# Cross-attention and mixture-of-experts kernel: how the setup fetches the head scales and the key and query weights, and when GpSimd clears the values' tiles

## The chip, the cores and the metric

The kernel runs on one core of one Trainium2 chip. The metric is the device time of one execution in microseconds (us); the time before is the median of three runs. The profile is one further execution, recorded by the hardware profiler, with times counted from the start of its span.

## The reference, cut to what matters

`x` is (4, 1024, 256), the context (4, 77, 256), the head values `f` are (4, 16), one number for each batch and head.

```python
def xattn(ctx, x_normed, f):               # 16 heads of 64
    k, v = split(layernorm(ctx, ln1_w, ln1_b) @ Wkv)
    q = layernorm(x_normed, ln2_w, ln2_b) @ Wq
    q = q * (1 + f[:, None, :, None]) + f[:, None, :, None]
    a = softmax(q k^T / 8)                 # by batch and head, over the 77 keys
    return (a v) @ Wout

x = x + xattn(ctx, norm(x), f)
x = x + experts(norm(x))                   # 9 experts, top 2 of a softmax router
```

All arithmetic is float32.

## The kernel before, in words

The order of the instructions on each engine is the order in which the program writes them down; the framework adds the waits on semaphores. Nothing is reordered by a scheduler. So an instruction that waits holds up everything written after it on the same engine.

The work has three stages. The **setup**, from 0 to about 67 us, folds the weights into per-batch matrices: `g` (queries' and keys' weights and the normalised context, so that scores come straight from the normalised tokens) and `u` (values times the output weights). The **attention** stage then runs over 32 sub-tiles of 128 tokens, and the **experts'** stage over blocks of token lists. The change touches only the first 27 us of the setup.

What the setup does there, by engine and line:

- SyncE issues the transfers of the context `cx` (L384, two halves), the keys' weights `wk_sb` and the queries' weights `wq_sb` (L389, two transfers each, one for each half of the 1024 columns), the values' weights `wv_sb` (L390) and the output weights `wo_sb` (L391). They run on queue q1.
- ScalarE issues, on queue q10, the two rows of the context's norm weights `crows` (L361), then `fs` (L367), the 64 head values copied to all 128 partitions, and later `wrow` (L476). Its arithmetic here is small roots, a quarter of `cn`, and one half of `cT` (L504).
- GpSimd clears and sends a few small tiles, then clears `vbd` (L590, 128 x 4096), `vrem` (L597) and parts of `u` (L599). An added dependency makes the clearing of `vbd` wait for the last instruction that writes the normalised context `cn` (L466) on VectorE. Iotas and small clears follow.
- TensorE runs eight warm-up products on zeros (L159) in two parts, turns `crows` (L424, into `pc`), and turns the normalised context `cn` into two tiles `pct` (L495), one for each half `c` of the 256 channels.
- VectorE takes the statistics of `cx` (L410, L412), makes `cn` (L466) and `cwb` (L475), copies `fs` into `shift` with two instructions, one for even and one for odd heads (L484), makes `scale1` and `shift` of it (L486, L487), clears `cfold` (L489), and then writes the second half of `cT` (L499), the normalised and weighted context. In the text `cT` has two halves: `c = 0` is ScalarE's (L504), `c = 1` is VectorE's (L499).
- The key loop (L512 to L529) has 8 blocks `n`. Each makes `pk` = `wk_sb` x `cT` in a PSUM bank, with two products (`c = 0` and `c = 1`) that the profile shows as two records each. ScalarE copies it to `kT` (L519) and VectorE multiplies it with `scale1` into `kTs` (L520). From block 4 on, TensorE also turns a quarter of `wq_sb` (L434, `pwq`) and VectorE multiplies it with `wrow` (L447).
- Then come `pcq` (L537), 32 products `pgk` (L651), and the values' part, in which `vbd` and `vrem` are written from `pv` (L724) and used by `pu` (L739) and `pur` (L745).

PSUM has 8 banks of 512 floats in a partition. `bank_tile` gives them out in turn, so a product has to wait until the tile eight places before it has been read.

## Time and profile before

| what | value |
|---|---|
| time before, median of 3 runs | 930.13 us (929.72 to 930.16) |
| the profiled execution | 929.22 us, of which its span 927.2 us |
| mean granted TensorE clock over the span | 0.994 |
| TensorE busy | 907.9 us (98% of the span) |
| VectorE, ScalarE, GpSimd busy | 453.3, 341.6, 318.9 us |
| chain of work that ended last | TensorE 87%, DMA 5%, issue 3%, VectorE 2% |
| VectorE waits for `fs` | 2.1 us, once |
| TensorE waits at `pk` (L515) | 2.6 us for `wk_sb`, 2.5 us behind VectorE's L489 and L499 |
| first `pk` products start | 10.11 us (the first two records), 13.41 us (all others) |

The profiled execution lies 0.91 us under the median. The line numbers are those of the kernel before. A busy share is a mean over stages; in the stretch that the change touches, TensorE is idle for several microseconds. "Idle before" in a timeline is the time that an engine had nothing running ahead of the instruction, with what released it.

### The profile page before, as it was taken

Reading aid. Unit: us, or ns where it says so; the run is one execution under the profiler, and the core shown is the slowest. Engines: PE = TensorE matmul, PEld = TensorE weight load, DVE = VectorE, ACT = ScalarE, POOL = GpSimd, SP = SyncE. Lnnn points to the kernel's source line nnn. Section 1 sums busy time; section 2 is a strip of 40 time slices with the busy share of each in tenths; the row PEclk is TensorE's granted clock in tenths of the full one; section 3 lists DMA queues with packets and bytes.
Section 4 is the critical chain, followed back from the end, with each engine's and each line's share of the span. In section 5 each row is a group of like instructions: output and inputs, shape, how many; then the busy total and the mean of one; then the engine's idle time right before and its main releaser. Section 6 shows DMA issues by size and latency. Waiting matters only on the chain.

```text
span 927.2 us, 13369 instructions
## 1 busy us (share of the span) xinstructions
PE 907.9 (98%) x4208; PEld 704.1 (76%) x4208; DVE 453.3 (49%) x1331; ACT 341.6 (37%) x1075; POOL 318.9 (34%) x329
## 2 busy tenths in 40 slices
PE   7999999999999999999999999999999999999996
PEld 5676767777777777788887777777778778778885
DVE  5777678788888977853632222222222222222221
ACT  2667565755656575551111222222222111112210
POOL 5000000412404151246544435435435435444422
PEclk8999999999999999999999999999999999999998
DMA  6100010503012610446869779779779777779822
GB/s 216 48 23 1 1 69 24 35 35 46 24 46 62 220 46 24 117 121 168 213 187 294 210 211 307 216 204 312 222 212 308 225 213 213 226 216 311 233 33 23
DMA packets 109747, 137.05 MB, mean 148 GB/s; under 512 B 24357, under 2 KB 79149, under 8 KB 109678
## 3 DMA queue, kind: packets, MB, share of 16 engines
q1 hardware_dynamic: 92042, 118.78, 41.6%
q0 software_dynamic: 17344, 17.26, 10.4%
q8 instruction: 34, 0.56, 0.3%
q14 instruction: 35, 0.29, 0.1%
q10 hardware_dynamic: 292, 0.17, 0.1%
HBM read 119.51 MB, written 18.33 MB: 149 GB/s over the span
## 4 chain that ended last, share of the span: by engine, by line
PE 87%; DMA 5%; issue 3%; DVE 2%; ACT 1%; POOL 1%; SPq 0%; POOLq 0%; ACTq 0%
PE pg L1193 21%; PE po L1267 16%; PE po L338 15%; PE psc L261 14%; PE pa L319 3%; PE psg L1229 3%; PE psu L1229 3%; PE psb L1229 2%; DMA out_dram<-co,ids 2%; PE px L1179 2%; PE pu L739 1%; PE pk L515 1%; PE ph L1250 1%; DMA wd_r<-in_L_ffn_Wd_dram 1%; PE pgk L651 1%
## 5 line engine op out<-in xcount | busy, mean ns | idle before, releaser
L1193 PE MATMUL pg<-xT,wgu 128*128 128x256 f32 x1144 | 251.7, 379 | 0.4 <-DMA wd_r<-in_L_ffn_Wd_dram 0.4
L1193 PEld LDWEIGHTS pg<-xT,wgu 128*128 128x128 f32 x1144 | 215.9, 190 | 29.3 <-issue 0.8
L1267 PE MATMUL po<-wd,hid 128*128 128x256 f32 (+1 forms) x804 | 180.5, 379 | 0.0
L1267 PEld LDWEIGHTS po<-wd,hid 128*128 128x128 f32 (+1 forms) x804 | 147.2, 187 | 21.3 <-issue 0.7
L275 ACT ACTIVATE ex<-psc,mx 128x77 f32<-128x77 f32 x512 | 124.1, 361 | 102.2 <-DVE mx L265 98.0
L1302 POOL DMA_INDIRECT out_dram<-co,ids x63 | 100.7, 1598 | 172.3 <-DVE co L1270 133.2
L918 POOL DMA_INDIRECT list_d<-r_entry,r_pli x64 | 68.2, 1065 | 255.4 <-issue 125.4
L338 PE MATMUL po<-u,aT 128*128 128x265 f32 x640 | 151.7, 391 | 0.9 <-ACT aT L327 0.6
L261 PE MATMUL psc<-g,zT 128*128 128x462 f32 (+1 forms) x384 | 139.1, 511 | 1.2 <-ACT zT L250 1.2
L338 PEld LDWEIGHTS po<-u,aT 128*128 128x128 f32 x640 | 118.7, 189 | 23.7 <-ACT aT L327 1.9
L1200 DVE TENSOR_TENSOR hid<-pg,sl 128x256 f32<-128x256 f32 x130 | 55.1, 425 | 160.1 <-ACT sl L1199 160.0
L1199 ACT ACTIVATE sl<-pg 128x256 f32<-128x256 f32 x130 | 49.8, 384 | 218.3 <-PE pg L1193 213.2
L261 PEld LDWEIGHTS psc<-g,zT 128*128 128x128 f32 x384 | 72.5, 189 | 59.2 <-issue 49.4
L1270 DVE TENSOR_SCALAR co<-po,ids 128x256 f32<-128x256 f32 x67 | 32.4, 484 | 136.0 <-PE po L1267 133.7
L1151 POOL DMA_INDIRECT yin<-y_d,ids x67 | 70.3, 1049 | 23.8 <-issue 15.1
L265 DVE TENSOR_REDUCE mx<-psc 128x6 f32<-128x462 f32 (+1 forms) x96 | 55.7, 581 | 17.9 <-PE psc L261 15.3
L295 DVE TENSOR_REDUCE sm<-ex 128x16 f32<-128x1232 f32 x32 | 45.9, 1435 | 37.0 <-ACT ex L275 37.0
L327 ACT COPY aT<-pa 128x512 f32<-128x512 f32 (+1 forms) x96 | 49.4, 552 | 26.4 <-PE pa L319 26.4
L319 PEld LDWEIGHTS pa<-ident,an 128*128 128x128 f32 x320 | 36.9, 141 | 7.7 <-PE po L338 1.4
L319 PE MATMUL pa<-ident,an 128*128 128x128 f32 x320 | 40.2, 273 | 1.0 <-DVE an L299 1.0
L299 DVE TENSOR_TENSOR an<-ex,rs 128x1024 f32<-128x1024 f32 x32 | 39.2, 1225 | 1.1
L1255 ACT COPY hid<-ph 128x384 f32<-128x384 f32 x15 | 7.2, 479 | 73.9 <-PE ph L1250 73.9
(310 smaller groups left out, 845.6 us busy)
## 6 DMA issues: line engine op xcount, KB each, us to landing
wgu<-in_L_ffn_Wg_dram SPq DMA_DIRECT2D x41, 704.0 KB
wd<-in_L_ffn_Wd_dram SPq DMA_DIRECT2D x41, 640.0 KB
wgu<-in_L_ffn_Wu_dram SPq DMA_DIRECT2D x41, 512.0 KB
wgu<-in_L_ffn_Wu_dram SPq DMA_DIRECT2D x41, 128.0 KB
x<-in_x_dram SPq DMA_DIRECT2D x8, 512.0 KB
out_dram<-x SPq DMA_DIRECT2D x8, 512.0 KB
y_d<-y SPq DMA_DIRECT2D x8, 512.0 KB
w<-in_L_ffn_Wg_dram SPq DMA_DIRECT2D x5, 704.0 KB
```

The source lines that it names most:

```text
L261: nc.tensor.matmul(psc[:, :w], zT[:, c, :], g_sb[i // NS // GPB][:, c, h * J : h * J + w], start=(c == 0), stop=(c == C - 1),)
L265: nc.vector.tensor_reduce(nmx[i][:, h : h + n], psc[:, : n * J].rearrange("p (h j) -> p h j", h=n), AX.X, ALU.max, negate=True,)
L275: nc.scalar.activation(exs[i][:, h + q, :], pscs[k][:, q * J : (q + 1) * J], AF.Exp, bias=nmx[i][:, h + q : h + q + 1],)
L319: nc.tensor.transpose(pa[:, q * P : (q + 1) * P], ans[i][:, (k + q) * P : (k + q + 1) * P], ident)
L338: nc.tensor.matmul(po[:, :DE], aT[:, n, :], u_sb[b][:, n, :], start=(n == 0), stop=(n == KC - 1))
L918: i = nc.gpsimd.indirect_dma_start(out=list_d[:, :], out_offset=bass.IndirectOffsetOnAxis(ap=place_i[:, s : s + 1], axis=0), in_=entries[k ...
L1151: return nc.gpsimd.indirect_dma_start(out=dst, out_offset=None, in_=src, in_offset=bass.IndirectOffsetOnAxis(ap=offsets, axis=0), **kw,)
L1193: nc.tensor.matmul(pg[:, g, :], w[:, c, at : at + P], xT[:, c, :], start=(c == 0), stop=(c == C - 1),)
L1200: nc.vector.tensor_tensor(hid[:, f, :], pg[:, 1, :], sl, ALU.mult)
L1229: nc.tensor.matmul(pgs[k][rows, :n], xT[:, c, rows], w[:, c, at : at + n], start=(c == 0), stop=(c == C - 1),)
L1267: nc.tensor.matmul(po[rows, :D], hid[:, f, at], d[:, f, :], start=(f == 0), stop=(f == NF))
L1302: i = nc.gpsimd.indirect_dma_start(out=out_r, out_offset=bass.IndirectOffsetOnAxis(ap=rows_of(j, h, rows), axis=0), in_=cos[j][:, h, :], i ...
```

## The change

It edits the setup in four places.

1. The transfer `fs` to 128 partitions goes. In its place ScalarE's queue brings `frows`, two partitions (even heads, odd heads) of 32 numbers each, picked from DRAM with a step of two numbers; it is issued ahead of the first activation instead of behind it. VectorE makes a small tile `two` from the identity matrix, and TensorE makes `pfs` = `two` x `frows`, which puts the head values on all 128 partitions in PSUM. `scale1` and `shift` are then made straight from `pfs`.
2. `scale1`, `shift` and the clearing of `cfold` move on VectorE from ahead of the second half of `cT` to behind it; the two copies of L484 go. `pfs` takes one turn of the PSUM banks between `pct` and `pk`.
3. `wk_sb` and `wq_sb` come in one transfer each, with rows of 1024 numbers in place of 512.
4. The clearing of `vbd` on GpSimd, and with it what follows there, waits for the second half of `cT` (L499) in place of the last of `cn` (L466).

```diff
+        frows = kside.tile([2, B, NP], F32, name="frows")
...
+        nc.scalar.dma_start(out=frows, in_=fside.rearrange("b (n t) -> t b n", t=2))
...
-        fs = vside.tile([P, B, NP, 2], F32, name="fs")
-        nc.scalar.dma_start(
-            out=fs.rearrange("p b n t -> p (b n t)"),
-            in_=fside.rearrange("(o b) h -> o (b h)", o=1).to_broadcast([P, B * H]),
-        )
...
-        wk_v = wkv[:, :INNER].rearrange("(c p) n -> p c n", p=P)
-        for dst, src in ((wk_sb, wk_v), (wq_sb, wq_v)):
-            for k in range(2):
-                at = slice(2 * k * quarter, 2 * (k + 1) * quarter)
-                nc.sync.dma_start(out=dst[:, :, at], in_=src[:, :, at])
+        nc.sync.dma_start(out=wk_sb, in_=wkv[:, :INNER].rearrange("(c p) n -> p c n", p=P))
+        nc.sync.dma_start(out=wq_sb, in_=wq_v)
...
+        two = kside.tile([2, 2, P // 2], F32, name="two")
+        nc.vector.tensor_copy(two, ident[:2, :2].unsqueeze(2).to_broadcast([2, 2, P // 2]))
...
-                normed = nc.vector.tensor_scalar(
+                nc.vector.tensor_scalar(
                     cn[:J, b, :], cx[:J, b, :], cmv[:J, b, 0:1], cr[:J, b : b + 1],
...
-        shift = kside.tile([P, NP, B], F32, name="shift")
-        scale1 = kside.tile([P, NP, B], F32, name="scale1")
-        for t in range(2):
-            half = slice(64 * t, 64 * t + 64)
-            nc.vector.tensor_copy(shift[half], fs[half, :, :, t].rearrange("p b n -> p n b"))
-        nc.vector.tensor_scalar(scale1, shift, ATT_SCALE, ATT_SCALE, ALU.mult, ALU.add)
-        nc.vector.tensor_scalar(shift, shift, ATT_SCALE, None, ALU.mult)
-        cfold_all = kside.tile([P, NP, P // QT], F32, name="cfold")
-        nc.vector.memset(cfold_all, 0.0)
...
-                nc.vector.tensor_scalar(
+                normed = nc.vector.tensor_scalar(
                     cT[:, c, :], pt[:, : B * J], cwb[:, c, 0:1], cwb[:, c, 1:2],
...
+        pfs = bank_tile("pfs")
+        nc.tensor.matmul(
+            pfs[:, : B * NP], two.rearrange("r t p -> r (t p)"),
+            frows.rearrange("r b n -> r (b n)"), start=True, stop=True,
+        )
+        heads = pfs[:, : B * NP].rearrange("p (b n) -> p n b", b=B)
+        nc.vector.tensor_scalar(scale1, heads, ATT_SCALE, ATT_SCALE, ALU.mult, ALU.add)
+        nc.vector.tensor_scalar(shift, heads, ATT_SCALE, None, ALU.mult)
+        cfold_all = kside.tile([P, NP, P // QT], F32, name="cfold")
+        nc.vector.memset(cfold_all, 0.0)
```

More of the change, by code (lines that the diff above doesn't have):

```diff
@@ L478 @@
         )
-        shift = kside.tile([P, NP, B], F32, name="shift")
-        scale1 = kside.tile([P, NP, B], F32, name="scale1")
-        for t in range(2):
-            half = slice(64 * t, 64 * t + 64)
-            nc.vector.tensor_copy(shift[half], fs[half, :, :, t].rearrange("p b n -> p n b"))
-        nc.vector.tensor_scalar(scale1, shift, ATT_SCALE, ATT_SCALE, ALU.mult, ALU.add)
-        nc.vector.tensor_scalar(shift, shift, ATT_SCALE, None, ALU.mult)
-        cfold_all = kside.tile([P, NP, P // QT], F32, name="cfold")
-        nc.vector.memset(cfold_all, 0.0)
-        cfold = cfold_all[:, :, : 2 * B].rearrange("p n (t b) -> p n t b", t=2)
         for c in range(C):
@@ L507 @@
                 )
+        shift = kside.tile([P, NP, B], F32, name="shift")
+        scale1 = kside.tile([P, NP, B], F32, name="scale1")
+        pfs = bank_tile("pfs")
[8 more added lines that the diff above has]
+        nc.vector.memset(cfold_all, 0.0)
+        cfold = cfold_all[:, :, : 2 * B].rearrange("p n (t b) -> p n t b", t=2)
         TURN = NP - NP // 2
```

## The prediction, on record before the changed kernel ran

> **What bounds the kernel now.** I read the page first, then TensorE's waits, then the chain of waits over the setup, then the timeline of the first 20 us, then its windows with clock and DMA. The page says that TensorE is the bound as a mean:

> ```profile
> PE 907.9 (98%) x4208; PEld 704.1 (76%) x4208; DVE 453.3 (49%) x1331; ACT 341.6 (37%) x1075; POOL 318.9 (34%) x329
> ```

> TensorE's waits, longest first, show where the missing 2% lie. The two longest are both at the first key products; the rest of the list is 1.5 us of start-up and 4.0 us spread over the kernel.

> ```profile
> PE pk L515 <- DMA wk_sb<-in_L_xattn_Wkv_dram: 2.6, 1, 2.6
> PE pk L515 <- DVE cfold L489: 2.5, 1, 2.5
> ```

> The chain over the setup (start, duration, what) says what ends there last: the transfer of `fs`, four small VectorE instructions, then TensorE without a break to 66.66 us.

> ```profile
> 1.69 7.38 DMA fs<-in_fside_Bx_dram
> ...
> 9.10 1.38 DVE shift L484
> 10.49 0.92 DVE shift L484
> ...
> 11.44 0.94 DVE scale L486
> ...
> 12.41 0.92 DVE shift L487
> ...
> 13.41 7.17 PE pk L515 x18
> 20.58 0.44 PE pwq L434 x4
> ```

> The timeline shows why such small instructions take 0.9 us each:

> ```profile
> 6.94 3.51 POOL L590 MEMSET vbd<- 128x4096 f32 x1 [1.38 <-DVE cn L466]
> 10.39 0.99 POOL L597 MEMSET vrem<- 128x1024 f32 x1
> 11.32 1.97 POOL L599 MEMSET u<- 128x1060 f32 x2
> ...
> 12.77 0.56 DVE L499 TENSOR_SCALAR cT<-pct,cwb 128x308 f32<-128x308 f32 x1
> ```

> VectorE's four end at 10.48, 11.41, 12.38 and 13.33; GpSimd's first two clears end at 10.45 and 11.38, the last at 13.29, and the pair's middle is 12.3. Each small instruction ends when a clear ends. The same kind of work without a clear beside it is short: L556 on 64x32 takes 0.18 us at 29.50. `cT` (c = 1) could have been written from 7.53, when `pct` was turned, but stands behind them and ends at 13.33.

> The windows (length, then busy times, clock, DMA share, GB/s) give the clock: it falls to half at about 11.1 and is back at about 18.0.

> ```profile
> 10.00:11.00 1.00, 0.76 (x2) 0.30 (x2) 0.99 (x2) 0.00 (x0) 1.00 (x2) 1.00 1.06 408
> 11.00:12.00 1.00, 0.00 (x0) 0.00 (x0) 0.96 (x2) 0.00 (x0) 1.00 (x2) 0.57 1.06 404
> ...
> 17.00:18.00 1.00, 1.00 (x3) 0.66 (x2) 0.48 (x1) 0.31 (x1) 0.00 (x0) 0.51 0.70 240
> 18.00:19.00 1.00, 1.00 (x5) 0.72 (x5) 0.00 (x1) 0.42 (x1) 0.00 (x0) 1.00 0.38 129
> ```

> At half clock a `pk` record comes every 0.51 us (weight loads at 14.09, 14.60, 15.11); at full clock every 0.26 (chain: 1.04 for 4).

> **The change, part by part.**

> *Removed from VectorE's path.* The wait for `fs` until 9.07 and the four instructions from 9.10 to 13.33. `cT` (c = 1) now starts when `pct` is turned (7.53) and takes 0.56: ready at 8.1. ScalarE's half is ready at 7.91 as before. `scale1` and `shift` come behind it; at 0.18 each they end near 8.6, and if they too had to sit out the clear of `vbd` and then `vrem`, near 12.7. That costs nothing either way: the first reader is `kTs` of block 0, and TensorE needs the bank of `pfs` back only eight tiles after it, at the second `pwq`, some 7 us into the products.

> *Added.* `two`: about 0.18 us, in VectorE's 0.36 us wait for ScalarE's root (5.18 to 5.54); were it held by GpSimd to 5.56, `cT` would be 0.2 later, which the next item hides. `pfs`: two small records, 0.2 us (as L424's) on an idle TensorE. Its wait for `frows` is the one that matters: all `pk` products stand behind it. Issued ahead of the activation, it delays the root's table load by 0.4 us, with 2.1 us of idle ScalarE behind it.

> *When `frows` lands.* No row shows a picked transfer of single numbers on this queue. The trace's landing marks (semaphore steps, one for each DMA engine that takes part) are 16 for a transfer to 128 partitions, 11 for `cx` (77 partitions), 1 for a row of `crows`; so two partitions will use one or two engines, 32 numbers or more each, where `fs` had 8 packets. `crows` landed at 3.56. `fs` landed engine by engine from 3.78 to 9.07, the first half of `wk_sb` from 5.68 to 9.98. The late engines are late for both queues, so they start late; they aren't slow at `fs`. Once going, a packet on this queue takes 15 ns (51 packets for 4.9% of 16 engines between 3 and 4 us), and one of `wk_sb` 82 ns (162 for 82.9% between 8 and 9). Twenty-four numbers more than `fs`, each perhaps behind one packet of weights, add 0.4 to 2.4 us: 4.2 at the earliest, 11.5 on the latest engine. I take 8.6, a middle engine (6.2 + 2.4).

> *The weights in one transfer.* TensorE had the first half at 10.11 (marks to 9.98), the second half landed by 11.37. Now block 0 needs all of it. If the number of packets set the pace, the whole lands like the first half, 9.98; if bytes do, like the second, 11.37 less what `fs` took; at 12.7 if one more half's time (1.34) is lost. Between 9 and 13 us the DMA moved 401 to 411 GB/s, whatever the packets' size, so bytes count late; before 8 us it moved at most 231, so there something else does. I take 11.0, near the bytes' end. `wq_sb` is needed by `pwq`, 6 us after the start; its last mark was 15.21: hidden. It would cost only beyond 17.

> *GpSimd* starts to clear at 8.15 instead of 6.94 and is done at 16.6 instead of 15.42. `vbd` is first written from `pv`, after 38.5; `numbers` reads the iotas in the thirties: hidden by 20 us. Nothing is queued behind it until the `z` clears, which wait for `pb` at 37.

> *The sum.* Products start at max(8.1, `pfs` at 8.8, 11.0) = 11.0 and are 20 records instead of 18, because none runs ahead. TensorE is then idle from 7.53 (bar `pfs`) to 11.0. With the clock's steps where this profile has them (half from 11.1; the next step up one interval earlier, 14.56, since 11.14 to 17.97 is two equal intervals of 3.41 and the first is now full), 7 records run to 14.56 and 13 more take 3.4: `pwq` at 17.95 instead of 20.58, 2.6 us earlier. From there TensorE's chain has no gap to 66.66, all else in the setup is driven by it, and it waits 4.0 us in all for the rest of the kernel, so the 2.6 us pass to the end. The profiled execution of 929.22 us would be 926.6; it lies 0.91 under the median of 930.13, and on the median the forecast is 927.5 us.

> With 9.98 as the start, `pwq` comes at 16.9 (gain 3.7); with 11.4 at 18.15 (2.4); with 12.7 at 18.9 (1.7).

> **The rivals.** *The clock takes the gain.* TensorE's idle stretch ends earlier, but the clock may stay at half for two intervals after the new start, 11.0 to 17.97: 13.6 records by then, 6.4 at 0.26, `pwq` at 19.6, gain 0.95: 929.2 us. For it: the steps need not fall where this profile has them. Against: the interval before (14.56 to 17.97) was full and did release the clock. [...]

> *The clock never falls*, because 3.5 us of idleness cover no whole interval: 20 records at 0.26 from 11.0, `pwq` at 16.2, gain 4.4: 925.7 us. Against: an interval with 0.76 us of work in it let the clock fall here.

> *The weights come late*, 12.5 to 12.7: gain 1.9 to 1.7, 928.2 to 928.4, as worked out above.

> *`frows` is late: slower.* The products stand behind a transfer of single numbers on few engines. Products from 12.9 on give no gain (10 records at 0.51 to 17.97, 10 at 0.26 to 20.58); with `pfs` 0.2, that is a landing at 12.7, or 0.29 us for each of 32 numbers after 3.56. At 0.45 us each they land at 18.0; `pwq` comes at 25.1, 4.5 us later: 934.6 us. For it: `fs` needed up to 7.0 us for 8 packets on an engine, 0.87 each. Against: the late engines' time was start-up, and 15 ns is the packet's own time. [...]

> That the change doesn't do what it says I give no chance of its own: the removed row on the chain is plainly replaced.

> **How the numbers follow.** Forecast case (weights between 9.9 and 12.4, one interval at half clock) 0.58, gain 1.9 to 3.7; clock never falls 0.07; clock takes the gain 0.17; weights late 0.07; `frows` late 0.11. What a measurement of this kernel can tell from no change is about 0.2%, 1.9 us. Faster by more than that: 0.58 + 0.07 = 0.65; within: 0.17 + 0.07 = 0.24; slower: 0.11. The range reaches from a gain of 4.2 (start at 9.5, or most of the case in which the clock stays up) to one of 0.2, below the case of the clock: 925.9 to 929.9. It leaves out the late `frows` and the tails.

> **What would show it.** Right: the chain over the setup without `fs` and without L484 to L487; `cT` (c = 1) done at about 8.1; the clear of `vbd` starting just after; TensorE's wait at `pk` put down to `wk_sb` until about 11; half clock for about 3.4 us; first `pwq` near 18 us; later stages shifted as a whole. Wrong: a long wait of TensorE at `pfs` for `frows`; `scale1` ending with the clear of `vbd` would only show that a PSUM source doesn't free VectorE from GpSimd; half clock until 18 would show the clock's rival; a gain at `pwq` that is gone at 67 us would mean that a wait in the values' part took its place.

## The result, and the profile after

The changed kernel took 925.42 us (median of 6 runs, 924.44 to 926.78). All six runs of before that stood beside it give 929.47 us (928.38 to 930.16), so the ratio is 0.9958 with an interval of 0.9945 to 0.9971: 4.05 us faster. The forecast was 927.5 us. Of the 2.1 us between the two, 0.7 is the base (the three runs of before shown ahead had a median of 930.13), and 1.4 is a gain larger than the 2.6 us that the sum gave. The profiled execution of the changed kernel took 924.82 us with a span of 922.8: 4.4 us less than that of before.

The page's row of TensorE in the changed kernel: two records more (`pfs`), 1.2 us less of busy time, and the same 98% share.

```profile
PE 906.7 (98%) x4210; PEld 703.5 (76%) x4210; DVE 450.0 (49%) x1330; ACT 341.7 (37%) x1075; POOL 318.2 (34%) x329
```

TensorE's waits of the changed kernel (us, times, longest): where two waits of 2.6 and 2.5 us stood at the first key products, one is left, and it is the weights'.

```profile
PE pk L515 <- DMA wk_sb<-in_L_xattn_Wkv_dram: 1.8, 1, 1.8
```

The timeline of the changed kernel (start, duration, engine, line, what, and in brackets the idle time before it and its releaser):

```profile
7.73 0.70 PE L479 MATMUL pct<-ident,cn 77*128 77x77 f32 x8
...
8.36 0.40 PE L497 MATMUL pfs<-frows,two 2*128 2x32 f32 x2
8.47 0.60 DVE L483 TENSOR_SCALAR cT<-pct,cwb 128x308 f32<-128x308 f32 x1 [1.11 <-PE pct L479]
8.98 0.18 DVE L503 TENSOR_SCALAR scale<-pfs 128x32 f32<-128x32 f32 x1
...
9.13 3.51 POOL L590 MEMSET vbd<- 128x4096 f32 x1 [3.56 <-DVE cT L483]
...
10.60 5.42 PE L515 MATMUL pk<-cT,wk_sb 128*128 128x308 f32 x20 [1.83 <-DMA wk_sb<-in_L_xattn_Wkv_dram]
...
15.85 0.60 PE L431 MATMUL pwq<-ident,wq_sb 128*128 128x128 f32 x4
```

`pfs` waits for nothing, `cT` (c = 1) starts the moment the last `pct` is done, `scale1` takes 0.18 us, the clear of `vbd` comes behind `cT`, and the products wait for `wk_sb` alone. They start at 10.60. Twenty records then take 5.42 us, 0.27 each, and the first `pwq` starts at 15.85. In before's timeline that row is:

```profile
20.42 0.60 PE L434 MATMUL pwq<-ident,wq_sb 128*128 128x128 f32 x4
```

So it comes 4.57 us earlier. The first scores start at 62.80 for 67.37, again 4.57, and the last product `pg` of the experts at 909.00 for 913.40, 4.40: the gain is made before 16 us and passes to the end.

The windows of the changed kernel (length, busy PE, PEld, DVE, ACT, POOL, then the granted clock, the DMA share and GB/s) over the stretch where before's clock stood at half:

```profile
11.00:12.00 1.00, 1.00 (x6) 0.72 (x5) 0.00 (x0) 0.09 (x1) 1.00 (x1) 1.00 1.03 408
...
17.00:18.00 1.00, 1.00 (x7) 0.77 (x7) 0.77 (x3) 0.47 (x2) 0.51 (x15) 1.00 0.51 170
```

The clock is 1.00 in both and in those between, where before's was 0.57 falling to 0.50 until 18. The half clock that the forecast charged didn't come in this execution. The six times fall into two groups: 924.44, 924.65 and 924.82 with a mean granted clock of 0.997 to 0.998, and 926.03, 926.38 and 926.78 with 0.995 to 0.996. The profiled execution belongs to the first; the second is taken up under the experiments.

### The profile page after: what moved, and what is told of

Its sections match the earlier page's. It is cut to its first block, busy times and chain, and to the rows that moved or that the text cites. A ratio compares the mean times of both kernels' runs of the same rounds, so it can differ in the third digit from the quotient of the medians.

```text
span 922.8 us, 13371 instructions
## 1 busy us (share of the span) xinstructions
PE 906.7 (98%) x4210; PEld 703.5 (76%) x4210; DVE 450.0 (49%) x1330; ACT 341.7 (37%) x1075; POOL 318.2 (34%) x329
## 3 DMA queue, kind: packets, MB, share of 16 engines
q0 software_dynamic: 17344, 17.26, 10.5%
## 5 line engine op out<-in xcount | busy, mean ns | idle before, releaser
L265 DVE TENSOR_REDUCE mx<-psc 128x6 f32<-128x462 f32 (+1 forms) x96 | 55.7, 581 | 18.1 <-PE psc L261 15.1
```

The costliest lines, as they stand in the source:

```text
L265: nc.vector.tensor_reduce(nmx[i][:, h : h + n], psc[:, : n * J].rearrange("p (h j) -> p h j", h=n), AX.X, ALU.max, negate=True,)
```

## The experiments

Gains are against the runs of before that stood beside each kernel on the same chip; the brackets hold the ratio's interval. Lines of these kernels are shifted by a few against those of the two kernels shown.

**Before, in the new order.** The block of `shift`, `scale1` and `cfold` goes behind `cT`; `fs`, the halves and the early clears stay.

```diff
-        for t in range(2):
-            nc.vector.tensor_copy(shift[half], fs[half, :, :, t]...)
-        nc.vector.tensor_scalar(scale1, shift, ...)
-        nc.vector.tensor_scalar(shift, shift, ...)
         for c in range(C):
             ...cT...
+        for t in range(2):
+            nc.vector.tensor_copy(shift[half], fs[half, :, :, t]...)
+        nc.vector.tensor_scalar(scale1, shift, ...)
+        nc.vector.tensor_scalar(shift, shift, ...)
```

> The kernel before, with one thing of the change: the making of shift, scale1 and the clear of cfold stands on VectorE behind the second half of cT. The fs transfer, the halves of the weights and GpSimd's early clears stay. Theory A (start of the key products, then clock): cT is ready near 8.1 us, the products start when the first half of the key weights lands (10.0 to 10.1 instead of 13.4); the small instructions still end with the clears (10.5 to 13.3), hidden by the PSUM banks. Gain 3.4 us less the 0.5 us of two records that ran ahead, plus 0 to 2.5 us of clock: 924.5 to 926.5 us against 929.5, no slower than the whole change. Rival B (VectorE has to be free of GpSimd, so the later clears are needed): kTs of block 0 comes after 13.4 and TensorE stalls for banks, less than 1 us gained. Rival C (the gain comes from fewer, longer transfers): no gain, 929.5 us.

Measured: 923.67 us against 928.84, 5.2 less, 0.9947 [0.9934, 0.9959], somewhat more than the 3.0 to 5.0 that theory A gave it. Its timeline:

```profile
6.98 3.51 POOL L590 MEMSET vbd<- 128x4096 f32 x1 [1.42 <-DVE cn L466]
...
9.08 0.60 DVE L487 TENSOR_SCALAR cT<-pct,cwb 128x308 f32<-128x308 f32 x1 [2.09 <-PE pct L483]
9.59 1.85 DVE L501 COPY shift<-fs 64x32 f32<-64x32 f32 x2
9.96 5.42 PE L515 MATMUL pk<-cT,wk_sb 128*128 128x308 f32 x20 [0.92 <-DMA wk_sb<-in_L_xattn_Wkv_dram]
...
11.48 0.93 DVE L503 TENSOR_SCALAR scale<-shift 128x32 f32<-128x32 f32 x1
```

The copies and `scale1` are still as long as in before (two in 1.85 us, one in 0.93), but TensorE doesn't wait for them now. `cT` reads PSUM and takes 0.60 us in the middle of the clear of `vbd`. The order alone gives all that the change gave, and the products start at 9.96, when the first half of the weights is there. That the product from `pfs` or the whole transfers were needed for the gain falls.

**Before, with late clears.** Only the instruction that the clear of `vbd` waits for is another: `cT` in place of the last `cn`.

```diff
-                normed = nc.vector.tensor_scalar(
+                nc.vector.tensor_scalar(
                     cn[:J, b, :], ...
...
-                nc.vector.tensor_scalar(
+                normed = nc.vector.tensor_scalar(
                     cT[:, c, :], ...
```

> The kernel before, with one thing of the change: GpSimd's clear of vbd waits for the second half of cT. Order on VectorE, fs and the halves stay. Theory A: after fs lands (9.07 us) the four small instructions take 0.2 us each instead of 0.9, cT is ready near 10.5, the products run from then: gain 2.9 us plus 0 to 2.5 us of clock, 924.5 to 926.7 us. Rival B' (the wait for fs is what counts, the blocking is not real and the instructions are slow by themselves): cT at 13.3 as before, no gain, 929.5 us. Rival C (transfers): no gain.

Measured: 922.64 us (922.29 to 923.07), 6.2 less, 0.9932 [0.9919, 0.9944], above the 2.9 to 5.4 that my theory gave it. Its timeline:

```profile
8.95 0.38 DVE L484 COPY shift<-fs 64x32 f32<-64x32 f32 x2 [2.06 <-DMA fs<-in_fside_Bx_dram]
9.36 0.18 DVE L486 TENSOR_SCALAR scale<-shift 128x32 f32<-128x32 f32 x1
...
9.99 5.42 PE L515 MATMUL pk<-cT,wk_sb 128*128 128x308 f32 x20 [1.55 <-DMA wk_sb<-in_L_xattn_Wkv_dram]
10.42 3.51 POOL L590 MEMSET vbd<- 128x4096 f32 x1 [4.86 <-DVE cT L499]
```

With no clear beside them the same four instructions take 0.18 to 0.2 us each, in the old order, behind the same `fs`; in before, beside the clears, they took 0.92 to 1.38. So in before the cost was the clears beside instructions that read and write SBUF, and either remedy alone, the order or the clears, takes it away. Beside the clears the source makes a difference, as the new order above has it: `scale1`, 32 columns from SBUF, took 0.93 us, and `cT`, 308 columns from PSUM, 0.60. By what mechanism a clear holds an instruction from SBUF, no view shows.

**Before, with filling products.** Twelve products of zeros into a bank of their own keep TensorE busy until VectorE's `cT` is there.

```diff
+        spare = bank_tile("spare")
+        for _ in range(12):
+            nc.tensor.matmul(spare[:, :D], idle[:, :P], idle, start=True, stop=True)
```

> The kernel before, with 12 products on zeros (5.3 us at full clock) on TensorE between pct and pk, into a bank of their own that nobody reads. Nothing else changes, and the key products can't start before 13.3 us. Theory A with the clock as the missing term: the clock stays up, the 3.4 to 6.8 us at half clock behind 13.4 are gone: gain 1.7 to 2.5 us, 927.0 to 927.8 us, and pwq at about 18.1 us instead of 20.6. Rival D (the clock is a by-product, the setup is bound by something else behind TensorE): 929.5 us or slightly more.

Measured: 927.08 us, 1.76 less, 0.9981 [0.9972, 0.9990]. Its timeline, TensorE alone:

```profile
7.93 5.39 PE L511 MATMUL spare<-u 128*128 128x256 f32 x24
13.15 5.35 PE L519 MATMUL pk<-cT,wk_sb 128*128 128x308 f32 x20
18.34 0.60 PE L434 MATMUL pwq<-ident,wq_sb 128*128 128x128 f32 x4
```

The products still start only behind VectorE's `cT`, at 13.15, but `pwq` comes at 18.34 for 20.42: 2.08 us in this profile, 1.76 in the time. This is nearly all the clock, with two small things that cancel in part: the products start 0.26 us earlier than in before's profile, and 20 records stand behind the wait instead of 18, which costs 0.52. The clock alone, 18 records in 7.01 us there against 0.26 a record here, is 2.34. Against it stands `pwq` at 15.85 in the changed kernel, 2.49 earlier again: of the 4.57 us, some 2.1 come with the clock alone and 2.5 with the earlier start.

The same profile shows what held VectorE in before:

```profile
6.63 3.51 POOL L594 MEMSET vbd<- 128x4096 f32 x1 [1.07 <-DVE cn L466]
6.71 4.39 DVE L484 COPY shift<-fs 64x32 f32<-64x32 f32 x2
```

`fs` landed at 6.69 here, 2.4 us earlier than in before's profile, and yet `cT` was done at 13.02 for 13.33. The first of the two copies took 3.46 us instead of 1.38 and ended, as in before, just behind the clear of `vbd` (10.17 behind 10.14, there 10.48 behind 10.45). In the next run `fs` landed at 7.97, and the copy ended at 10.28, behind a clear that ended at 10.25. So the clears alone set when `cT` was ready in before; the transfer `fs`, with which the chain begins there, was hidden behind the first of them.

**Before, with whole transfers.** One transfer each for `wk_sb` and `wq_sb`, nothing else.

```diff
-        for dst, src in ((wk_sb, wk_v), (wq_sb, wq_v)):
-            for k in range(2):
-                nc.sync.dma_start(out=dst[:, :, at], in_=src[:, :, at])
+        nc.sync.dma_start(out=wk_sb, in_=wkv[:, :INNER]...)
+        nc.sync.dma_start(out=wq_sb, in_=wq_v)
```

> The kernel before, with one thing of the change: key and query weights in one transfer each. Theory A: the products wait for cT (13.3 us) as before, the weights are there by 10.5; only the two records that ran ahead at 10.1 may go or stay: 929.2 to 930.0 us, no difference. Rival C (the gain of the change comes from its transfers): 925.5 to 927 us.

Measured: 928.85 us, no difference, 1.0000 [0.9991, 1.0009]. Its timeline, TensorE alone:

```profile
10.08 0.76 PE L512 MATMUL pk<-cT,wk_sb 128*128 128x308 f32 x2 [2.19 <-DMA wk_sb<-in_L_xattn_Wkv_dram]
...
13.21 7.63 PE L512 MATMUL pk<-cT,wk_sb 128*128 128x308 f32 x18 [2.38 <-DVE cT L496]
```

The weights are hidden behind VectorE's late `cT` here, whole or in halves, so this part of the change is worth nothing as long as that wait stands.

**Changed, with filling products.** Four products of zeros into spare columns of `pfs`'s bank.

```diff
+        for _ in range(4):
+            nc.tensor.matmul(pfs[:, D : 2 * D], idle[:, :P], idle, start=True, stop=True)
```

> The changed kernel, with 4 products on zeros (1.8 us at full clock) on TensorE between pct and pfs, into spare columns of the bank of pfs. Theory A with the clock as the missing term: the changed kernel's times fall in two groups, about 924.6 and 926.4, because its 1.8 us of idle TensorE sometimes, and sometimes not, cost one interval at half clock (3.41 us, so 1.7 us of time). With the gap filled the slow group goes: median 924.4 to 924.9 and a spread under 1 us. Rival D (the two groups come from something else, the DMA's start for one): median 925.4 and both groups as before.

Measured: 924.60 us (924.14 to 925.05) against 928.53, 3.9 less, 0.9961 [0.9947, 0.9975]. The ratio is the changed kernel's own; what differs is the spread. The changed kernel's six runs fall into two groups, around 924.6 and 926.4, 1.8 apart; these fall into one, 0.9 wide. The clock's marks in the traces of before and of the changed kernel lie multiples of 3.413 us apart; half clock over one such interval costs half of it, 1.7 us by estimate, so the upper group is probably executions in which the clock did fall. The granted clocks of the runs agree: one such interval lowers the mean over 922 us by 0.0019, the upper group has 0.995 to 0.996 where the lower has 0.997 to 0.998, and all six runs here have 0.997 or 0.998. No profile of that upper group was taken.

**Changed, with halves.** `wk_sb` and `wq_sb` in two transfers each again.

```diff
-        nc.sync.dma_start(out=wk_sb, in_=wkv[:, :INNER]...)
-        nc.sync.dma_start(out=wq_sb, in_=wq_v)
+        for dst, src in ((wk_sb, wk_v), (wq_sb, wq_v)):
+            for k in range(2):
+                nc.sync.dma_start(out=dst[:, :, at], in_=src[:, :, at])
```

> The changed kernel, with key and query weights in two halves each as before. Theory A (the pace of the DMA before 8 us is set by start-up, not by packets): the first half lands at 9.9 to 10.1 instead of 10.5, and the second by 11.4, in time for block 4: gain of 0.3 to 0.6 us, 924.8 to 925.2 us. Rival E (packets set the pace): the halves land as in the kernel before or later, and block 4 or the query weights wait: 925.4 to 926.5 us.

Measured: 922.65 us (922.09 to 923.04), 5.9 less, 0.9940 [0.9926, 0.9954]. I had expected 0.3 to 0.6 us over the changed kernel. Its timeline, TensorE alone:

```profile
8.02 0.40 PE L500 MATMUL pfs<-frows,two 2*128 2x32 f32 x2
8.52 5.45 PE L518 MATMUL pk<-cT,wk_sb 128*128 128x308 f32 x20
...
13.80 0.60 PE L434 MATMUL pwq<-ident,wq_sb 128*128 128x128 f32 x4
```

The first half landed at 6.87 us, so the products follow `pfs` after 0.1 us, and `pwq` comes 2.05 us ahead of the changed kernel's; the clock stays up. On the same chip the changed kernel with filling products, whose transfers are whole, took 924.60, with its products from 10.75, behind the zeros and 0.37 us after the weights: no run of one reaches into the runs of the other, though the intervals of the two ratios overlap a little.

**Changed, with halves and filling products**: the last two edits together.

> The changed kernel, with the halves of the weights and the 4 products on zeros together. If both help, as theory A has it: 924.0 to 924.5 us with a spread under 1 us, faster than the changed kernel by 0.9 to 1.4 us. Under rival D or E: 925.4 us or more.

Measured: 923.95 us, 4.6 less, 0.9954 [0.9940, 0.9968], 1.3 slower than the halves alone. The first half landed at 7.08, but the products started at 10.05 for 8.52: the zeros and `pfs` run from 7.85 to 10.12, so the zeros themselves are now what the products wait for. That the two help each other fell.

**Changed, with early clears.** The clear of `vbd` waits for the last `cn` again, as in before.

```diff
-                nc.vector.tensor_scalar(
+                normed = nc.vector.tensor_scalar(
                     cn[:J, b, :], ...
...
-                normed = nc.vector.tensor_scalar(
+                nc.vector.tensor_scalar(
                     cT[:, c, :], ...
```

> The changed kernel, with GpSimd's clear of vbd waiting for cn as before, so that the clears run from about 7.3 us, beside cT, scale1 and shift. Theory A1 (a VectorE instruction that reads PSUM doesn't wait for a clear): scale1 and shift take 0.18 us, cT is ready near 9.1: same time, 925.4 us. Theory A2 (any VectorE instruction waits for the clear of 3.5 us): cT ends with it near 10.8, the products start 0.2 us later or more, and scale1 and shift end with the next clears; 925.6 to 926.5 us.

Measured: 924.28 us (922.63 to 928.55), 4.25 less, 0.9953 [0.9939, 0.9968]: the changed kernel's own. The profile fell on the slowest run, 928.55. Its timeline and its windows:

```profile
7.07 3.51 POOL L590 MEMSET vbd<- 128x4096 f32 x1 [1.51 <-DVE cn L463]
8.99 0.60 DVE L483 TENSOR_SCALAR cT<-pct,cwb 128x308 f32<-128x308 f32 x1 [1.91 <-PE pct L479]
11.24 0.60 PE L497 MATMUL pfs<-frows,two 2*128 2x32 f32 x2 [2.29 <-DMA frows<-in_fside_Bx_dram]
...
11.77 8.35 PE L515 MATMUL pk<-cT,wk_sb 128*128 128x308 f32 x20
11.88 0.19 DVE L503 TENSOR_SCALAR scale<-pfs 128x32 f32<-128x32 f32 x1 [2.29 <-PE pfs L497]
...
19.95 0.60 PE L431 MATMUL pwq<-ident,wq_sb 128*128 128x128 f32 x4
```

```profile
11.00:12.00 1.00, 0.76 (x3) 0.73 (x4) 0.12 (x2) 0.00 (x0) 1.00 (x2) 0.50 1.00 400
```

Two things stand here. `scale1` and `cT` read PSUM and take 0.19 and 0.60 us beside the clears of `u` (two in 1.90) and of `vbd` (3.51), so in the changed kernel the later clears are worth nothing that these runs can tell: its VectorE instructions no longer need them. And this execution is two of the prediction's rivals at once: `frows` landed at 11.10, the products stood behind it, and the clock fell at 10.82 (0.91 granted from 10 to 11 us, 0.50 from 11 to 12); `pwq` at 19.95 is 4.1 us behind the changed kernel's profile. A second profile of the same kernel asked whether the early clears made `frows` late:

> The changed kernel with GpSimd's early clears once more, for a second profile: in the first, frows landed at 11.2 us on one of its two engines, where it landed at 4.1 to 5.8 in four other kernels. If the early clears are its cause, it lands after 9 us again and the products start behind it; if it is chance, at 4 to 6 us, and the products start with wk_sb at 10.4 to 10.9 us.

There `frows` landed at 5.87 and the products started at 10.77; the run took 926.75 us, on a chip where before took 931.20. So the early clears alone don't make `frows` late; and it landed at 10.65 in a kernel with late clears, the one with halves of `wq_sb` below. What makes it late is open.

**Which half it is.** Changed, with halves of `wk_sb` alone, with halves of `wq_sb` alone, and with all halves and the transfer `fs` added back, which nobody reads. They ran on another chip than the four before them, where before took 931.20 us.

> The changed kernel with the key weights alone back in two halves, the query weights in one transfer. Theory F (what the change loses is that block 0 has to wait for all of wk_sb, 10.4 to 10.9 us, where the first half alone lands near 7): products start behind pfs at 8.5 to 9.0 us, and the time is that of both in halves, 922.3 to 923.3 us. Theory G (the number of packets in flight slows all transfers, query weights included): only part of it, 923.8 to 925.0 us.

> The changed kernel with the query weights alone back in two halves, the key weights in one transfer. Theory F: nothing gained, the products still wait for all of wk_sb near 10.5 us: 925.0 to 926.0 us. Theory G: 923.8 to 925.0 us.

> The changed kernel with the weights in halves, and beside frows the transfer fs to 128 partitions as in the kernel before, which nobody reads. Theory H (the 128 packets of fs hold up the first half of wk_sb: with fs it landed at 8.4 to 10.0 us in four kernels, without at 6.9 and 7.1): the first half lands at 8.4 to 10.0 and the products start then: 0.3 to 1.5 us slower than the same without fs, 923.0 to 924.2 us. Rival (the landing differs by chance or by what else the kernels differ in): 922.3 to 923.0 us and a start at 8.5 us.

Measured: 925.91 (0.9940 [0.9923, 0.9957]), 926.68 (0.9949 [0.9930, 0.9969]) and 925.47 us (0.9935 [0.9918, 0.9952]). All three lie above what was expected, on a chip where before too was 2.7 us slower, and the intervals overlap, so the times don't decide between theories F and G. The starts of the products, 9.71 with halves of `wk_sb` alone and 11.09 with halves of `wq_sb` alone, decide little more, because the second is a late `frows`:

```profile
10.79 0.37 PE L499 MATMUL pfs<-frows,two 2*128 2x32 f32 x2 [1.97 <-DMA frows<-in_fside_Bx_dram]
```

The whole `wk_sb` had landed there at 10.28, 0.71 us after the first half in the other kernel. The first half landed at 9.57 with no `fs` and at 9.62 with it, so that `fs` delays the weights is not supported. Nor did the early landing at 6.87 come back on this chip.

**The changed kernel and the two best, side by side** on a chip where before took 930.60 us:

> The changed kernel itself, beside the two below on one chip. Theory A with the clock: key weights land at 10.3 to 10.9 us as in all five kernels with the whole transfer and without fs, products start then; times 3.6 to 4.5 us under the kernel before, in two groups some 1.7 us apart, by whether TensorE's idle time took the clock down. Theory K (the transfers are worth nothing either way, differences between calls were the chips): the same as the two below within 0.5 us.

> The changed kernel with both weights in halves, again. Theory F (the whole transfer costs what the changed kernel loses): first half by 7 to 9.6 us, products from 8.5 to 9.7, 0.8 to 2.8 us faster than the changed kernel. Theory K: within 0.5 us of it.

> The kernel before with GpSimd's later clears alone, again. Theory F: fs at 8 to 9 us, cT by 10.4, first half of the weights by 10.0, products from 10.0 without a gap: 0.4 to 1.5 us faster than the changed kernel. Theory K: within 0.5 us of it.

Measured: the changed kernel 927.86 us (12 runs, 924.94 to 929.66; 0.9968 [0.9955, 0.9981]), with halves 925.12 (924.54 to 925.59; 0.9938 [0.9924, 0.9952]), before with late clears 926.12 (922.21 to 926.77; 0.9942 [0.9923, 0.9961]). The timelines of the changed kernel and of that with halves:

```profile
11.17 5.42 PE L515 MATMUL pk<-cT,wk_sb 128*128 128x308 f32 x20 [2.14 <-DMA wk_sb<-in_L_xattn_Wkv_dram]
```

```profile
9.48 5.42 PE L518 MATMUL pk<-cT,wk_sb 128*128 128x308 f32 x20 [0.49 <-DMA wk_sb<-in_L_xattn_Wkv_dram]
```

The products start 1.69 us earlier with halves, and the time is 2.74 us less on the same chip: the intervals don't overlap, and theory K falls. The changed kernel's own 2.74 us under before is less than the 3.6 to 4.5 expected. Its twelve runs fall into six from 924.94 to 927.19 and six from 928.52 to 929.66; the profiled one, 927.19, is of the first six, and against them the halves gain 1.6 us on the mean, near the 1.69 of their earlier start. What makes the other six slower is open: their granted clocks, 0.996 to 0.998, hardly differ from the 0.997 and 0.998 of the first, so a fall of the clock explains two of them at most.

So whole transfers are the part of the change that costs. That it is the one of `wk_sb` follows from the waits: TensorE waits for `wk_sb` in both timelines, and never for `wq_sb`; the times of the two halves taken singly don't show it. The version with halves is faster than the changed kernel, and than before by 5.5 and 5.9 us on two chips. Before with late clears alone can't be told apart from it: 925.12 and 926.12, with overlapping intervals.

## Why the prediction was right and wrong

- **The removed wait: right in the main.** VectorE's path to `cT` was the one that ended last, and it is gone. Of its terms only the four instructions beside the clears counted; the wait for `fs` until 9.07 did not, as the run of before with filling products shows. `cT` was done at 9.07, not 8.1: `cx` landed 0.4 us later in this execution, `pct` had to stand behind a warm-up that half clock made longer, and ended at 8.43 for 7.53, and `cT` took 0.60. It was hidden, as said.
- **`scale1` and `shift`: 0.18 each, the lower of the two values given.** The execution with early clears settled which: `scale1` from PSUM took 0.19 us beside a clear of `u`, where from SBUF it had taken 0.94 beside the clears in before.
- **`two`: 0.18 us at 5.51, inside the wait for the root. Right.**
- **When `frows` lands: 8.6 was too late for most executions.** It landed with two marks, as those of `cx` and `crows` had it, at 4.97 and 5.55; in nine of eleven profiles at 4.1 to 5.9, in the two others at 10.65 and 11.10. The bounds, 4.2 and 11.5, were about the true ones, the middle between them was not the likely value, and the rival of a late `frows` exists; in the worst profile it left `pwq` only 0.5 us ahead of before's, and the run took what before took.
- **The weights in one transfer: 11.0 forecast, 10.46 landed, 10.60 started.** Seven profiles with a whole transfer have 9.94 to 11.04, about the bounds' span. I compared them with before's first half (9.98) and so found a cost of 1.1 us, a gain of 2.6 for 3.7. In the changed kernel with halves the first one landed at 6.87 and 7.08 on one chip, 9.34 and 9.57 on another: the comparison that counted was with what halves would give beside the rest of the change, and side by side that was 1.69 us at the start and 2.74 in the time.
- **The clock: the step that failed.** "7 records run to 14.56" at half clock charged 7 x (0.51 - 0.26) = 1.75 us that this execution did not pay. The gain at `pwq` was 4.57, not 2.63. The difference of 1.94 is these 1.75, and 0.40 from the start at 10.60 instead of 11.0, less 0.05 because the 20 records took 5.25 us up to `pwq` instead of 5.2, and less 0.16 because the chain's 20.58 is 20.42 in the timeline. It is the case "the clock never falls", which I gave 0.07; its gain of 4.4 is what the profile shows, and its time of 925.7 lay just outside my range. Judged by the granted clocks, the half clock that I took for nearly certain probably came in three of the six runs; in the other three, the profiled one among them, it didn't.
  The mistake lay in the idle stretch. I took TensorE's stops from before's profile, 7.53 to 11.0, and let only the start of the products move. In this execution `cx` came later, the warm-up's records came every 0.43 us through its whole first part, at half clock, which lasted until 6.27, the first mark of this trace's clock (in before until 4.32, with 0.22 a record from there), `pct` and `pfs` ended at 8.43 and 8.76, and TensorE was idle for 1.83 us, not 3.3. The marks at which the trace's clock changes lie whole multiples of 3.413 us apart, and begin at another place in each execution: in before at 4.32, 11.15, 17.97 and 922.51 (2, 2 and 265 times 3.413), here at 6.27 and 917.63 (267 times). Counted on from 6.27, such a mark at 9.69 cuts the idle stretch in two, and the intervals on both sides of it are 73% busy: the clock stayed. The interval from 7.73 to 11.15 in before was 22% busy, and the clock fell; that of the changed kernel's second profile, 6.9 to 10.3, was 62% busy, and it stayed. In the execution with early clears the clock fell after an interval of some 45% (7.41 to 10.82), so an interval with no work at all was not needed for the fall. With halves of `wq_sb` alone the clock stayed after one of 49% (7.14 to 10.56). The six warm-up records from 6.33 on agree with the starts at 6.9 and 7.14: they take 1.82 and 1.95 us there, and 1.56 in before at full clock.

  No run's profile shows the term itself, half clock for one interval alone: in before it lasted from 11.15 to 17.97 and in the execution with early clears from 10.82 to 17.64, 6.83 and 6.82 us; the changed kernel's profile has none there.

  Two smaller readings of the forecast are slightly off and change nothing: the half clock lasted 6.83 us, not 6.85, and one half's time was put at 1.34 us, where the halves' last marks, 9.98 and 11.37, lie 1.39 apart.
- **GpSimd later: hidden, as said.** The clears ended near 17.5 (16.6 forecast) for 15.42, with nobody waiting.
- **`wq_sb` whole: hidden, as said.** It landed at 14.14 and `pwq` needed it at 15.85.
- **2.6 us pass to the end: the passing was right.** 4.57 us at 16 and 63 us, 4.40 at 909. The 0.17 went in the experts' stage, probably at `px`, whose wait for its input is 0.16 longer here and differs by up to 1.1 us between executions of the kernels.

What stays open: why the first half of the weights lands anywhere from 6.9 to 10 us, why `frows` is late in some executions, and what the slower half of the changed kernel's twelve runs side by side is. That the upper group of its first six runs is the clock is argued from its distance, from the runs with filling products and from the granted clocks; no profile of that group shows where the clock fell.

## What to carry to other kernels

When a wait in front of a matmul stage is shortened, work out TensorE's whole idle stretch in each clock interval, with its start as free to move as its end: nearly half of the 4.6 us here was the clock, which in these traces changes only at marks a multiple of 3.413 us apart (2 to 267 times it). Where those marks will fall isn't known ahead (the first stood at 4.32 in before, at 6.27 in the changed kernel), so both cases need a chance of their own. A small instruction that lasts five times its like, 0.92 us for 0.18 here, is to be read beside what the other engines run at that moment; moving either the instruction or the clear beside it gave as much as the whole change. And the part that a stall hides (halves or whole, no difference in before) is to be costed again without the stall: there it was 1.7 us at the start of the products and 2.7 in the time.
